# Who reads the output's, k's and q's products out of PSUM: ScalarE alone, with VectorE's share added in SBUF

## The chip, the cores and the metric

One core of a Trainium2 chip runs the whole program. The metric is the device time of one execution in microseconds, as a median of runs. Engines are named as the profile names them: PE (TensorE's matmuls), PEld (its weight loads), DVE (VectorE), ACT (ScalarE), POOL (GpSimd) and SP (SyncE, which here only issues DMAs).

## The reference

Two attention blocks are applied in turn to 8 images of 512 channels and 32 x 32 positions (S = 1024 tokens), all in float32.

```
for each of the two layers:
    xn  = group_norm(x, 8 groups)                  # over channels and positions
    q, k, v = Wq xn + bq, Wk xn + bk, Wv xn + bv   # 512 x 512 matrices
    for each of 8 heads (64 channels):
        a   = softmax(q^T k / 8) over the 1024 keys
        out = a v
    x = x + Wp out + bp
```

## The kernel before

**Jobs.** One image in one layer is a job; there are 16, in the order image 0 layer 0, image 1 layer 0, image 0 layer 1, image 1 layer 1, then the next two images. They are counted from 0. A job's life is: v products (`v_phase`), a phase of products that this text calls the deep phase (`deep_phases`), attention (`Attention.run`), and then the next job's v products. The deep phase of job n computes the output projection of job n - 1 and then k and q of job n. Job 0's has only k and q. `DEEP_V` is 99, so v never runs in the deep phase, and everything that the code does under `with_v` or `n >= DEEP_V` is not reached.

**Products.** Each 512 x 512 by 512 x 1024 multiplication is done with a seven-product scheme (Strassen's, in Winograd's form), applied twice. The outer seven are *chains*, the inner seven are the products of a chain: one matmul of 128x128 weights on 128x256 each, which the profile shows as two records. A deep phase has 21 chains (O, K, Q, seven each in the order `OUTER` = 1, 2, 6, 5, 7, 3, 4), so 147 products. Chains are counted from 0 to 20 here. Two chains are interleaved: product j of chain c stands at place 7c + 2j.

**One chain** has four PSUM banks, z, y, u and w, and takes its products in the order 1, 5, 6, 2, 7, 3, 4 (`chain`, L497 and L501). Product 1 goes to z, and ScalarE copies z to y. Product 5 goes to w, and ScalarE copies it to a small SBUF tile `s5` (L827): this is the product shared by two quarters. Product 6 is added in z, and ScalarE copies z to u. Product 2 completes y, product 7 z, product 3 u and product 4 z again; after each of these four, `put` takes a quarter of the result out of PSUM. For products 2 and 4 ScalarE does it (L816, or L818 with a bias), for products 7 and 3 VectorE, which adds s5 in the same instruction (L823, or L825 with a bias). The next product that goes to a bank waits for the read before it. The last chain of a phase has an order of its own, and half of it goes another way (L820, L821).

**After a chain** (`end`), its result stands in a tile p of the pool `epool` or in its place in k or q. The outer seven results are added up on VectorE: `add` for p into p, k or q (L839), `more` for p into x (L888). Where `more` is called with `moved`, GpSimd issues a DMA that adds p into x (L886). A p tile is free after its last such use. `epool` has 12 buffers: six for p tiles (`PARTS`) and six for weights fetched ahead (`RING`, `fetch`, L188 and L194), which `used` asks for 2.5 us, by the kernel's own clock, after a chain's end.

**Order.** PE, ACT and DVE run in program order (`manual_schedule`), so where Python emits an instruction is where it runs on its engine. The kernel keeps a clock: 0.432 us for each product (`takes`), and `later` puts a step at a time on it. VectorE's work in a deep phase is emitted one item after each product 7 and 3: first `soon` (sums of the moving matrices: four `early` ones for k, then those of output chains 5 and 6, `outs.steps`), then `outer` (the additions above), then `extra`, which holds steps with the first chain at which they may run, such as the next normalisation's statistics (`reads`, from chain 15) and the next image's load (`load_x`, four DMAs at once, from chain 11). What is left of `extra` goes into the first steps of attention. `next_work` and `pump`, which choose by modelled times, are there but used only with `with_v`.

**Weight sums.** `prepare` makes the seven weight factors of a chain with four VectorE instructions (L161 to L167), two chains ahead, the first time that a layer's K and Q are used (jobs 0 and 2); afterwards they come from DRAM ready made (`w<-deep`).

Of the kernel before, what the change touches and what calls it, by code (L numbers as in the profile page):

```python
# [50 lines left out]
AHEAD, TAIL, SLACK, BEHIND, ADD = 0.8, 12.0, 0.6, 1.2, 1.24  # L51
PLACE = {2: (0, 0), 6: (0, 1), 5: (1, 1), 7: (1, 0)}
# [28 lines left out]
def fast_path(  # L81
# [116 lines left out]
    def prepare(key):  # L198
        if key not in raw:
            return  # L200
        raw.discard(key)
        n, which, o = key
        w = held[key]
        for part in range(4):
            factor(w, part)
        keep = wdram.tile([P, NW, P], F32, name=f"deep_{which}_{jobs[n][1]}_{o}")
        deep[which, jobs[n][1], o] = keep
        later(1.0, lambda: nc.sync.dma_start(keep, w))

# [45 lines left out]
    def load_x(b):  # L255
        for cc in range(NC):
            nc.sync.dma_start(xs[b][:, cc, :], x[b, cc * P : (cc + 1) * P, :])

# [375 lines left out]
    def deep_phases(n, extra, outs=None, early=()):  # L634
# [21 lines left out]
        def p_tile(key, name, uses):  # L656
            while len(holds) >= PARTS:
                assert values or outer
                next_work(len(chains), True)
# [6 lines left out]
        def next_work(c, forced=False, limit=None):  # L666
# [9 lines left out]
            if planned and planned[0][1] <= now and not forced:  # L676
                _, _, _, us, fn = planned.popleft()
            elif fits(shared):
# [48 lines left out]
        def begin(c):  # L727
# [7 lines left out]
            if c + 2 < len(chains):  # L735
                ahead, oo = chains[c + 2]
                prepare((job(ahead), ahead, oo))
            if which == O and not with_v and c in (3, 4):
                soon.extend(outs.steps(c + 2))
# [13 lines left out]
            while unread and unread[0] <= c - 3:  # L753
                next_work(c, True)
            s5 = small.tile([P, QT], F32, tag="s5", name=f"s5_{n}_{c}", bufs=3)
# [49 lines left out]
            def put(oo, ph, ps):  # L805
# [8 lines left out]
                if ph == 0:  # L814
                    if b is None:
                        nc.scalar.copy(to_, ps)  # L816
                    else:
                        nc.scalar.activation(to_, ps, AF.Identity, bias=b)  # L818
                elif ends and oo == 1:
                    nc.scalar.activation(to_, ps, AF.Identity, bias=b)  # L820
                    nc.vector.tensor_add(to_, to_, s5)  # L821
                elif b is None:
                    nc.vector.tensor_add(to_, ps, s5)  # L823
                else:
                    nc.vector.scalar_tensor_tensor(to_, ps, b, s5, ALU.add, ALU.add)  # L825
# [3 lines left out]
        def end(c):  # L829
            which, o = chains[c]  # L830
            m = job(which)
            used((m, which, o))
# [4 lines left out]
            def add(to_, a, b, frees):  # L837
                def go():
                    nc.vector.tensor_add(to_, a, b)  # L839
                    let_go((which, frees))  # L840

                ready[go] = clock[0] + BEHIND
                outer.append(go)

            if which == V:
                def add_five():
                    unread.remove(c)
                    to_ = p(o)[:, 2:4, :].rearrange("p t (o c) -> p t o c", o=2)
                    five = fives[V, o].rearrange("p (t c) -> p t c", t=2).unsqueeze(2)
                    nc.vector.tensor_add(to_, to_, five.to_broadcast([P, 2, 2, P]))  # L850

                def plus(to_, a):
# [4 lines left out]
                    ready[go] = clock[0] + BEHIND  # L857
                    values.append((ADD, go))

                unread.append(c)  # L860
                if c < 2:
                    add_five()
                    spend(0.72)
                else:
                    ready[add_five] = clock[0] + BEHIND
                    shared.append((0.72, add_five))
# [7 lines left out]
            if which == O:  # L874
# [3 lines left out]
                def more(oh, sh, part, moved=False):  # L878
# [20 lines left out]
                    ready[go] = clock[0] + BEHIND  # L899
# [12 lines left out]
                elif o == 6:  # L912
                    add(p(6), p(6), p(1), 1)
# [4 lines left out]
                elif o == 7:  # L918
                    add(p(7), p(7), p(6), 6)
# [7 lines left out]
            for to_, a in {  # L927
                2: ((2, 1),), 6: ((6, 1),), 7: ((7, 6), (6, 5), (5, 7)), 3: ((6, 3),), 4: ((7, 4),),
            }.get(o, ()):
                add(p(to_), p(to_), p(a), a)  # L930
# [3 lines left out]
        soon, outer = deque(early), deque()  # L934

        def thunk(i, c, j):
            def go():
                if with_v and not began:
                    began.append(clock[0])
                    free_at[0] = clock[0] + TAIL  # L940
# [4 lines left out]
                if with_v:  # L945
                    if chains[c][0] != V and order[j] in (7, 3):
                        spend(0.38)
                    pump(c, limits[i] and clock[0] + limits[i])
                elif order[j] in (7, 3):
                    if soon:  # L950
                        soon.popleft()()
                    elif outer:
                        outer.popleft()()
                        while outer and outer[0] in free:
                            outer.popleft()()
                    elif extra and extra[0][0] <= c:
                        extra.popleft()[1]()
                if j == 6:
                    end(c)
                    if c + 1 == len(chains):  # L960
                        while outer:
                            outer.popleft()()
                        assert not shared and not values and not planned
# [20 lines left out]
        for c, j in reversed(at):  # L984
            limits.append(limit)
            if chains[c][0] != V and (LAST_ORDER if c + 1 == len(chains) else ORDER)[j] == 7:
# [549 lines left out]
    for n in range(-1, len(jobs)):  # L1536
        last = n + 1 == len(jobs)
        outs = None
        if n >= 0:
# [46 lines left out]
            else:  # L1586
# [7 lines left out]
                elif n >= DEEP_V:  # L1594
                    for i, fn in enumerate(reads):
                        put(3 + i, fn)
                    at = (18, 25, 26, 28, 30, 31, 33, 35, 37, 39)
# [12 lines left out]
                if n + 1 >= DEEP_V:  # L1610
                    for at, fn in zip((41, 43, 45, 47, 49, 51, 53, 55), deep_first):
# [5 lines left out]
                def begin_plan():  # L1617
                    extend_plan(n + 1)
                    for _ in range(RING):
                        fetch()  # L1620

                put(61 if n + 1 < DEEP_V else 56, begin_plan)
# [314 lines left out]
```

## Time and profile before

| what | value |
|---|---|
| median of 3 runs | 3215.66 us (3212.3 to 3217.05) |
| the profiled execution | 3215.82 us, of which the span is 3214.0 us |
| TensorE busy | 3188.8 us (99%), granted clock 0.998 |
| VectorE busy | 2519.1 us (78%) |
| ScalarE busy | 1912.8 us (60%) |
| GpSimd busy | 278.9 us (9%) |
| DMA | 426.45 MB, mean 133 GB/s |
| one deep phase, job 4 | 63.1 us (828.0 to 891.1) |
| one attention, job 4 | 110.0 us (891.1 to 1001.1) |
| v products, job 4 | 24.7 us (803.3 to 828.0) |

How to read it: a line of a timeline has the start in us from the span's start, the length in us, the engine, the line of the kernel, the operation, the tiles written and read, and the shape; in brackets, how long the engine was idle before it, and what ended that. A line of the groups has the shape, the count, the busy time in all, the mean in ns, and the idle time before it with what ended it. A line of the sums by window has the window, its length, the busy time of PE, PEld, DVE, ACT and POOL with the number of instructions, the granted clock, the share of the DMA engines and GB/s. Matmul records overlap: the next starts before the one before it ends, so the pace is the distance between starts.

### The profile page before, as it was taken

To read this page: it belongs to the slowest core of one execution; us is meant where nothing else is said; L and a number is where in the kernel's file an instruction comes from. 1 tells how busy PE (TensorE), PEld (TensorE's weight loads), DVE (VectorE), ACT (ScalarE), POOL (GpSimd) and SP (SyncE) were. 2 spreads that over 40 slices of the span, in tenths; PEclk is the share of its full clock that TensorE was granted. 3 is DMA by queue.
4 is the path that set the end of the run, shared out by engine and by line. 5 is a ranking of instruction groups with operands and counts; after the bars stand their busy time and mean duration, and the time that the engine had idled before them with its cause. 6 is when DMAs were issued, how large, how long until landed. Compare 5 with 4: busy or idle time off the path is not lost.

```text
span 3214.0 us, 58182 instructions
## 1 busy us (share of the span) xinstructions
PE 3188.8 (99%) x22917; PEld 1868.0 (58%) x22917; DVE 2519.1 (78%) x3718; ACT 1912.8 (60%) x3063; POOL 278.9 (9%) x318
## 2 busy tenths in 40 slices
PE   9999999999999999999999999999999999999998
PEld 7366384663846638366483754837557374573844
DVE  8697897867878688786887878778787787877857
ACT  4746646466565665656656565565656656566563
POOL 0100001001010000100001000010000100001000
PEclk9999999999999999999999999999999999999999
DMA  7646565555645354455554535446446463445643
GB/s 273 146 133 161 119 198 146 129 166 110 199 80 136 95 120 137 87 147 143 125 171 94 153 85 124 117 92 178 119 119 174 94 176 61 123 115 102 194 92 76
DMA packets 189561, 426.45 MB, mean 133 GB/s; under 512 B 37736, under 2 KB 63712, under 8 KB 189280
## 3 DMA queue, kind: packets, MB, share of 16 engines
q1 hardware_dynamic: 140432, 273.23, 26.4%
q0 software_dynamic: 48848, 149.44, 25.3%
q8 instruction: 181, 2.97, 0.4%
q14 instruction: 100, 0.82, 0.1%
HBM read 228.15 MB, written 43.84 MB: 85 GB/s over the span
## 4 chain that ended last, share of the span: by engine, by line
PE 90%; DVE 5%; DMA 3%; issue 1%; SPq 0%; ACT 0%; POOL 0%; DVEq 0%; ACTq 0%; POOLq 0%
PE sc L1097 25%; PE po L1148 25%; PE vd L800 10%; PE zd L800 10%; PE z L553 7%; PE yd L800 5%; PE ud L800 4%; PE y L553 2%; PE u L553 2%; PE v L553 2%; DVE acc L1118 1%; DMA x<-p 1%; DMA r<-r 1%; DVE acc L1128 1%; DMA deep<-round 0%
## 5 line engine op out<-in xcount | busy, mean ns | idle before, releaser
L1102 ACT ACTIVATE e<-sc 128x1024 f32<-128x1024 f32 x1024 | 1043.7, 1023 | 566.5 <-PE sc L1097 525.1
L1148 PE MATMUL po<-e,v 64*64 64x512 f32 x8192 | 1059.0, 590 | 2.2 <-ACT e L1102 2.2
L1097 PE MATMUL sc<-q,k 64*64 64x512 f32 x8192 | 1058.7, 590 | 0.0
L1148 PEld LDWEIGHTS po<-e,v 64*64 64x64 f32 x8192 | 313.5, 133 | 568.2 <-issue 544.5
L1097 PEld LDWEIGHTS sc<-q,k 64*64 64x64 f32 x8192 | 311.7, 133 | 562.1 <-issue 523.0
L1118 DVE TENSOR_TENSOR acc<-acc,e 128x1024 f32<-128x1024 f32 x320 | 390.6, 1221 | 67.0 <-ACT e L1102 60.0
L1116 DVE TENSOR_TENSOR acc<-e,e 128x1024 f32<-128x1024 f32 x128 | 156.8, 1225 | 255.1 <-ACT e L1102 255.0
L1125 POOL DMA_DIRECT2D e<-e x224 | 192.6, 860 | 1771.6 <-ACT e L1102 1364.4
L1128 DVE TENSOR_TENSOR acc<-acc,e 128x1024 f32<-128x1024 f32 x224 | 272.9, 1218 | 7.7 <-DMA e<-e 4.6
L800 PE MATMUL zd<-deep,w 128*128 128x256 f32 x860 | 242.1, 381 | 2.3 <-DVE p L823 1.9
L800 PE MATMUL vd<-deep,w 128*128 128x256 f32 x804 | 225.0, 381 | 2.8 <-DVE p L823 0.8
L800 PEld LDWEIGHTS zd<-deep,w 128*128 128x128 f32 x860 | 163.8, 191 | 26.3 <-DVE p L823 3.1
L800 PEld LDWEIGHTS vd<-deep,w 128*128 128x128 f32 x804 | 152.8, 191 | 25.6 <-DVE p L823 1.2
L1183 DVE TRANSPOSE_TENSOR_REDUCE r<-acc 128x32 f32<-128x1024 f32 x128 | 159.2, 1244 | 3.8
L886 POOL DMA_DIRECT2D x<-p x61 | 72.9, 1195 | 949.2 <-ACT p L816 669.7
L1171 DVE TENSOR_TENSOR q<-po,px 128x512 f32<-128x512 f32 x128 | 87.9, 687 | 73.2 <-ACT px L1169 71.7
L800 PE MATMUL vd<-os,w 128*128 128x256 f32 x420 | 117.7, 379 | 0.0
L553 PE MATMUL z<-w,t 128*128 128x256 f32 x480 | 111.0, 379 | 0.0
L553 PE MATMUL z<-w,xn 128*128 128x256 f32 x480 | 110.9, 385 | 0.0
L577 ACT COPY v<-z 128x512 f32<-128x512 f32 x32 | 18.7, 585 | 148.7 <-PE z L553 148.7
L553 PEld LDWEIGHTS z<-w,xn 128*128 128x128 f32 x480 | 90.8, 192 | 24.6 <-PE po L1148 11.4
L501 ACT COPY ud<-zd 128x256 f32<-128x256 f32 x156 | 55.7, 357 | 76.6 <-PE zd L800 75.6
(274 smaller groups left out, 4295.0 us busy)
## 6 DMA issues: line engine op xcount, KB each, us to landing
w<-deep SPq DMA_DIRECT2D x301, 448.0 KB, 4.5
e<-e POOLq DMA_DIRECT2D x224, 512.0 KB, 4.7
x<-p POOLq DMA_DIRECT2D x61, 512.0 KB, 6.3
rb<-rd SPq DMA_DIRECT2D x96, 256.0 KB, 3.8
w<-keep SPq DMA_DIRECT2D x76, 256.0 KB, 5.1
w<-wqkv_dram SPq DMA_DIRECT2D x57, 256.0 KB, 4.7
x<-x_dram SPq DMA_DIRECT2D x28, 512.0 KB, 4.8
out_dram<-x SPq DMA_DIRECT2D x28, 512.0 KB, 4.7
```

The costliest lines, as they stand in the source:

```text
L553: nc.tensor.matmul(ps[:, ti * CH : (ti + 1) * CH], right(src, tx[0], o)[:, cc, t0 : t0 + P], w[:, cc, :], start=(start and ti == 0 and cc ...
L800: nc.tensor.matmul(ps, lhs[:, FACTOR[i], :], moving[i], start=start, stop=True, skip_group_check=True,)
L886: nc.gpsimd.dma_start(to_, p(part), accum_op=ALU.add)
L1097: nc.tensor.matmul(sc[h * HD : (h + 1) * HD, j, :], k[r, hp, k0 : k0 + HD], q[r, hp, sh * HALF : (sh + 1) * HALF], start=True, stop=True,)
L1102: nc.scalar.activation(e, sc, AF.Exp, scale=SCALE)
L1116: nc.vector.tensor_add(acc[g], self.es[i - 1], e)
L1118: nc.vector.tensor_add(acc[g], acc[g], e)
L1125: nc.gpsimd.dma_start(self.summed[i], self.summed.pop(i - 1), accum_op=ALU.add)
L1128: nc.vector.tensor_add(self.acc[g], self.acc[g], self.summed.pop(i))
L1148: nc.tensor.matmul(po[g][j * HD : (j + 1) * HD, h, :], v[r, kc, d0 : d0 + HD], e[r, j, :], start=(kc == 0), stop=(kc == NT - 1),)
L1171: nc.vector.tensor_add(to_, p[:, 1, :], px)
L1183: nc.vector.tensor_reduce(self.r[:, 0, m, :], self.acc.pop(g).rearrange("p j (b e) -> p (j b) e", e=RP), AX.X, ALU.add, apply_transpose=True,)
```

## The change

It does four things. What stands under `with_v` or `n >= DEEP_V` is changed too but not reached, and is left out here.

1. `put`: ScalarE reads all four quarters out of PSUM, the two of products 7 and 3 without s5. Only in the last chain of a phase does it stay as it was.
2. `end`: a chain's s5 is now added by one VectorE instruction to both quarters at once in SBUF (`add_five`, 128x512). All that was done at a chain's end (additions into p, k, q and x, and the accumulating DMAs) is now called after `add_five` has been emitted (`follow`).
3. VectorE's work in every deep phase is chosen by `next_work`: items are emitted while the modelled end of what was emitted lies under 0.8 us (`AHEAD`) ahead of the kernel's clock. The order is `soon`, then `shared` (the `add_five` items, from 1.2 us after the chain's end), then `outer`, then `extra`; modelled prices are 0.75, 0.72, 1.24 and 0.65 us, and 0.9 for `prepare`. `soon` items that a chain needs, and an `add_five` that is three chains old (`FIVES`), are emitted at the latest when that chain begins.
4. The next image's load is four steps of one DMA each, from chains 15, 16, 17 and 18, still ahead of the statistics in `extra`.

```diff
@@ prepare
-            return
+            return False
...
         later(1.0, lambda: nc.sync.dma_start(keep, w))
+        return True
@@
+    def load_steps(b):
+        def chunk(cc):
+            if cc == 0:
+                x_tile(b)
+            nc.sync.dma_start(xs[b][:, cc, :], x[b, cc * P : (cc + 1) * P, :])
+        return [(15 + cc, lambda cc=cc: chunk(cc)) for cc in range(NC)]
@@ next_work
+            elif soon and not forced:
+                us, fn = 0.75, soon.popleft()[1]
             elif fits(shared):
                 us, fn = shared.popleft()
@@ begin
-                prepare((job(ahead), ahead, oo))
+                if prepare((job(ahead), ahead, oo)):
+                    spend(0.9)
             if which == O and not with_v and c in (3, 4):
-                soon.extend(outs.steps(c + 2))
+                soon.extend((c + 2, fn) for fn in outs.steps(c + 2))
+            while any(for_ <= c for for_, _ in soon):
+                soon.popleft()[1]()
+                spend(0.75)
@@ put
                 to_ = e[:, oo, ph * QT : (ph + 1) * QT]
                 b = bias(oo)
-                if ph == 0:
-                    if b is None:
-                        nc.scalar.copy(to_, ps)
-                    else:
-                        nc.scalar.activation(to_, ps, AF.Identity, bias=b)
-                elif ends and oo == 1:
+                if ends and ph == 1 and oo == 0:
+                    nc.vector.scalar_tensor_tensor(to_, ps, b, s5, ALU.add, ALU.add)
+                elif b is None:
+                    nc.scalar.copy(to_, ps)
+                else:
                     nc.scalar.activation(to_, ps, AF.Identity, bias=b)
+                if ends and ph == 1 and oo == 1:
                     nc.vector.tensor_add(to_, to_, s5)
-                elif b is None:
-                    nc.vector.tensor_add(to_, ps, s5)
-                else:
-                    nc.vector.scalar_tensor_tensor(to_, ps, b, s5, ALU.add, ALU.add)
@@ end
+            if c + 1 == len(chains):
+                follow(c)
+                return
+            def add_five():
+                unread.remove(c)
+                five = fives[which, o]
...
+                    to_ = tiles[which, o][:, :, QT:]
+                    five = five.unsqueeze(1)
+                    nc.vector.tensor_add(to_, to_, five.to_broadcast([P, 2, QT]))
+                follow(c)
+            unread.append(c)
...
+                ready[add_five] = clock[0] + BEHIND
+                shared.append((0.72, add_five))
+        def follow(c):
             which, o = chains[c]
             m = job(which)
@@ thunk
-                elif order[j] in (7, 3):
-                    if soon:
-                        soon.popleft()()
-                    elif outer:
-                        outer.popleft()()
-                        while outer and outer[0] in free:
-                            outer.popleft()()
-                    elif extra and extra[0][0] <= c:
-                        extra.popleft()[1]()
+                if c + 1 == len(chains) and order[j] in (7, 3):
+                    spend(0.45)
+                pump(c, limits[i] and clock[0] + limits[i])
                 if j == 6:
                     end(c)
                     if c + 1 == len(chains):
-                        while outer:
-                            outer.popleft()()
+                        while shared or values or outer:
+                            next_work(c, True)
@@ after each job's attention
             if jobs[n][1] == 1 and jobs[n][0] + 2 < B:
-                extra.append((11, lambda b=jobs[n][0] + 2: (x_tile(b), load_x(b))))
+                extra.extend(load_steps(jobs[n][0] + 2))
```

## The prediction

> **What bounds the kernel now.** I read first the page's busy times and chain:
>
> ```profile
> PE 3188.8 (99%) x22917; PEld 1868.0 (58%) x22917; DVE 2519.1 (78%) x3718; ACT 1912.8 (60%) x3063; POOL 278.9 (9%) x318
> PE 90%; DVE 5%; DMA 3%; issue 1%; SPq 0%; ACT 0%; POOL 0%; DVEq 0%; ACTq 0%; POOLq 0%
> ```
>
> TensorE is busy for 99% of a 3214.0 us span: nothing gains here unless it ends a TensorE wait. So I asked, in the stage that the change edits (output, k and q products, one phase for each job; jobs and chains count from 0), for sums by window: job 0, then jobs 1 to 5.
>
> ```profile
> 37.20:82.40 45.20, 43.03 (x196) 36.37 (x194) 41.90 (x106) 26.95 (x70) 0.00 (x0) 1.00 0.72 259
> 223.20:287.20 64.00, 63.36 (x293) 55.28 (x291) 48.45 (x80) 40.38 (x105) 4.79 (x4) 1.00 0.48 133
> 422.00:490.60 68.60, 65.37 (x293) 54.49 (x291) 61.98 (x144) 40.26 (x105) 4.77 (x4) 1.00 0.65 197
> 626.10:693.20 67.10, 65.16 (x293) 56.33 (x291) 47.49 (x79) 40.49 (x105) 5.99 (x5) 0.97 0.67 197
> 828.00:891.10 63.10, 63.10 (x293) 55.35 (x291) 48.39 (x80) 40.49 (x105) 4.77 (x4) 1.00 0.65 201
> 1025.80:1089.00 63.20, 63.20 (x297) 55.42 (x296) 48.44 (x80) 40.41 (x105) 4.77 (x4) 1.00 0.49 133
> ```
>
> The columns are length, then busy time of PE, PEld, DVE, ACT, POOL. Where nothing stalls, a phase takes 63.1 us for 146 products (two matmul records each), 0.432 us a product; jobs 4 to 15 are all within 0.2 us of that. Job 0 has 98 products, 42.3 us at that pace, and takes 45.2. The stage's whole loss is thus 2.9 + 0.9 + 5.5 + 4.0 = 13.3 us, 0.4% of the time, in four phases of sixteen. What ends the waits there, from TensorE's timeline of jobs 2 and 3 and the chain of waits of job 3:
>
> ```profile
> 441.11 0.70 PE L800 MATMUL zd<-os,w 128*128 128x256 f32 x2 [0.85 <-ACT yd L497]
> 448.89 0.70 PE L800 MATMUL zd<-deep,w 128*128 128x256 f32 x2 [0.63 <-DVE p L823]
> ...
> 649.13 11.51 DMA x<-p
> 660.66 3.80 DMA out_dram<-x
> ...
> 666.28 8.64 DMA w<-deep
> ...
> 674.97 0.80 PE vd L800 x2
> ```
>
> Jobs 0 and 2 wait for VectorE's late reads of PSUM (the second line is one of some twelve): VectorE also makes weight sums there and is busy 41.9 of 45.2 us and 62.0 of 68.6. Job 1 and the first line wait for ScalarE, which itself waits for a buffer. Job 3 waits for weights, queued on SP behind output stores, which wait for an 11.5 us accumulating DMA, and then behind the four loads of the next image.
>
> **The change, part by part.** *Reads of products 7 and 3.* Of each chain of seven products ScalarE read five and VectorE two; now ScalarE reads all seven (the last chain of a phase stays as it was). Rows of ScalarE's groups: 0.372 us for a copy, 0.473 with a bias. Two more of these in each of 20 chains are 20 x 2 x 0.43 = 17 us of ScalarE a phase, 40.5 + 17 = 57.5 of 63.1. That is close, so what matters is the distance between starts. Job 4, ScalarE's timeline:
>
> ```profile
> 847.18 0.47 ACT L818 ACTIVATE p<-vd,out_step 128x256 f32<-128x256 f32 x1
> 847.62 0.47 ACT L818 ACTIVATE p<-yd,out_bias 128x256 f32<-128x256 f32 x1
> 848.10 0.36 ACT L497 COPY yd<-zd 128x256 f32<-128x256 f32 x1
> ```
>
> Instructions of 0.47 us start 0.44 apart, at TensorE's pace, and one overlaps the next; in the whole trace the least distance after such a one is 0.37 us. One read per 0.432 us product fits. The Trainium skill (TensorEngine Tiling (Array Packing), section PSUM Bottleneck) says to use both ScalarE and VectorE for emptying PSUM, which speaks against this change and would make the sum that of rival (c). By the rows it fits, and I go by the rows. With the VectorE reads gone, so is their wait: 2.9 us in job 0 and 4.4 of job 2's 5.5. VectorE stays nearly as loaded in these two, and its lag now reaches TensorE through the three s5 tiles (three chains, some 9 us, of cover) and the weight sums (made two chains ahead, 6 us). I take 2.5 and 4.2; bounds 0 and 7.3 together.
>
> *The added sum.* VectorE adds s5 to 128x512 in SBUF. Nearest rows: 128x256 takes 0.419 us (p<-p,s) and 128x1024 1.216; on that line 0.69. It replaces two reads of 0.42 to 0.48: VectorE does 0.2 us less a chain, beside other work: 0. The quarter is now complete only after this add, so everything behind it is later by its wait and length, 0.06 + 0.69 = 0.75 us: the adds into k and q (not needed at once) and, on POOL's queue, the DMA that accumulates p into x. That matters at one place. In each ordinary phase chain 0's DMA goes first, chain 1's waits for it (same part of x), and chain 5 writes its first quarter into chain 1's p buffer. The row of that write, in the groups by form, and the write in job 5 and in job 2:
>
> ```profile
> L818 ACT ACTIVATE p<-yd,out_step 128x256 f32<-128x256 f32 x15 | 7.1, 473 | 6.5 <-DMA x<-p 3.3 <-PE ud L800 1.8 <-PE zd L800 1.0
> ...
> 1042.97 0.47 ACT L818 ACTIVATE p<-yd,out_step 128x256 f32<-128x256 f32 x1 [0.59 <-DMA x<-p]
> ...
> 440.31 0.47 ACT L818 ACTIVATE p<-yd,out_step 128x256 f32<-128x256 f32 x1 [1.80 <-PE ud L800]
> ```
>
> At pace it starts 16.6 us into a phase; chain 1's DMA lands 15.7 to 17.4 us in (jobs 3 to 15). In job 2 it started 1.74 us late (the DMA had landed at 440.2, whatever the line names) and TensorE's next gap was 1.0 us, the stall at 441.11; up to 0.7 us late, the other phases lose nothing. So about 0.73 us are tolerated. With both DMAs 0.75 us later, the landings of jobs 3 to 15 give starts of 16.6 to 18.2 us: seven of the thirteen exceed the tolerance by 0.45 to 0.85, plus 0.1 each to get going again, together 4.7 us. Job 2 loses 0.8 more. Bounds: 0, if the pool gives chain 5 another buffer (chain 0's is now free by then too, since its add no longer stands behind the output sums), and 25, if the DMAs move by 2.5 us. I take 5.5, the value of the nearest row. Job 1's wait is for the same kind of buffer, but there the add into x and with it the DMA come forward, from 16 us into the phase to about 9: 0.9 gained.
>
> *The order by modelled time.* VectorE's items enter its program when its modelled backlog is under 0.8 us, no longer one after each product 7 and 3. Adding the diff's own prices over a normal phase: 20 x 0.72 + 21 x 1.24 + 8 x 0.75 (four of them really 1.13 by the 1.22 us rows) + 9 x 0.65 + 0.9 = 53.2 of 63.5, so nothing is squeezed out, and the statistics, which now end partly in attention, end in the phase. Cost 0; the cover is VectorE's 14.7 idle us (63.1 - 48.4). In job 2 twelve further weight sums of 0.93 fill that room; eight statistics items are left to attention, and the group sums follow their gather after one step instead of five. There VectorE may wait for the gather's DMAs with attention's sums queued behind it: 0 to 2 us for TensorE, I take 0.5.
>
> *Next image in four parts.* Four DMA issues (0.42 us each on SP) leave their place ahead of five weight loads in job 3 and go, one a chain, to chains 15 to 18, behind nearly all weight loads of the phase. The 2 MB no longer share the DMA engines with the load that ended at 674.9. That load took 8.6 us; the median w<-deep takes 4.5. So it would land about 4 us earlier, or 5.9 with the 1.8 us of issues. The wait of 1.94 us goes. What follows it goes too:
>
> ```profile
> 675.55 1.92 PE L800 MATMUL zd<-deep,w 128*128 128x256 f32 x4
> 677.26 1.06 PE L800 MATMUL ud<-xn,w 128*128 128x256 f32 x2
> ```
>
> Four matmul records in 1.71 us are 0.43 a record, half pace, for some 3 us: 1.6 us lost. The skill (TensorE: Matmul & The Clock Gate, section Part 1: The HAM clock gate) puts the drop after an idle window of about 3.4 us; here a 1.94 us gap was followed by it. By the rule alone this part would bring 2.2 us, by the row 3.8. I take 3.5 of the row's. Each step is also charged 0.65 us to VectorE without work there: 2.6 us of its idle time in six phases, four statistics items moved into attention: 0.
>
> **Sum**, against the profiled 3215.8 us (span 3214.0 and 1.8 around it; the median of the runs is 3215.7, the same): 2.5 + 0.9 + 4.2 + 3.5 = 11.1 gained, 5.5 + 0.5 = 6.0 given back. 3215.8 - 5.1 = 3210.7.
>
> **Rivals.** (a) Chain 5 gets another buffer: the 5.5 vanish, and job 2's remaining 1.1 too: 3215.8 - 11.1 - 1.1 + 0.5 = 3204. For: the pool picks by who is free, and job 2's counterpart in job 1 got a weight's buffer. Against: jobs 3 to 15 all have the wait's pattern. (b) Slower, by the same buffer: the DMA of chain 1 lands over 2 us later, because the add on VectorE waits in order behind other items. With 2.5 us, thirteen phases lose 1.9 each: 25 - 11 = +14, 3230. It decides from landings at 18.4 us into the phase on average. Against: VectorE is through with its four first sums at 4.2 us, before chain 0 ends at 4.45. (c) ScalarE becomes the bound: if its 0.473 us reads did not overlap and each cost 0.07 between, a biased chain would take 4 x 0.54 + 3 x 0.43 = 3.45 us against 3.02, 12 chains in 15 phases: +77, 3290. The 0.44 us starts speak against it. (d) It does not do what it says: VectorE's lag in jobs 0 and 2 stalls TensorE through s5 and the weight sums as it did through PSUM, and the small gains meet the small losses: 3215.
>
> **How the numbers follow.** Forecast 0.46, (a) 0.22, (b) 0.17, (c) 0.03, (d) 0.12. 0.2% is 6.4 us, about what a measurement of this kernel can tell from no change: faster is below 3209.3. The forecast's own spread (3204 to 3217) puts two fifths there, (a) nearly all: 0.40 faster. Slower is (b), (c) and the forecast's tail: 0.21. The range from 3201 to 3224 leaves out (c), most of (b) and a little below.
>
> **What would show it.** Right: no TensorE wait for VectorE's p, k or q left at the products' line; job 0's phase near 42.7 us, job 2's near 65, job 3's near 63.6 with no wait for w<-deep; jobs 4 to 15 between 63.1 and 64, with short waits on yd where ScalarE waited for x<-p. Wrong: a phase of 63.1 everywhere (then a), over 64.5 in ordinary phases (b), ScalarE starts over 0.44 apart in a row (c), or stalls in jobs 0 and 2 that now name s5 or w (d).

## The result, and the profile after

| kernel | median | ratio to the kernel before, 95% |
|---|---|---|
| before, beside the first runs | 3214.6 us (6 runs) | |
| changed | 3231.7 us (6 runs) | 1.0051 [1.0038, 1.0064] |
| changed, in a later series | 3228.8 us (4 runs), before 3213.9 (21 runs) | 1.0042 [1.0027, 1.0058] |

The change makes the kernel about 16 us slower, where 5 us less were forecast; 3231.7 us lies above the range. The profiled execution took 3232.4 us (span 3230.6). Its busy times show the work that moved, as expected: ScalarE 1913 to 2160 us, VectorE 2519 to 2488.

```profile
PE 3192.1 (99%) x22917; PEld 1866.6 (58%) x22917; DVE 2488.1 (77%) x3405; ACT 2159.6 (67%) x3689; POOL 283.7 (9%) x318
```

The same sums by window as before the change: the deep phases of jobs 0, 2, 3, 4 and 5, and then job 2's attention (window, length, busy time of PE, PEld, DVE, ACT and POOL, clock, DMA share, GB/s).

```profile
38.60:80.50 41.90, 41.90 (x195) 36.54 (x193) 37.23 (x86) 36.44 (x96) 0.00 (x0) 1.00 0.80 280
422.90:487.60 64.70, 63.70 (x297) 54.95 (x295) 55.19 (x115) 53.85 (x145) 4.77 (x4) 1.00 0.70 208
632.80:695.90 63.10, 63.10 (x295) 55.19 (x293) 43.10 (x56) 56.27 (x145) 5.99 (x5) 1.00 0.70 209
830.60:893.70 63.10, 63.10 (x293) 55.24 (x292) 43.94 (x57) 56.46 (x145) 4.77 (x4) 1.00 0.66 201
1028.50:1095.70 67.20, 65.03 (x293) 56.28 (x291) 45.89 (x62) 56.30 (x145) 4.77 (x4) 0.97 0.47 125
487.60:605.40 117.80, 112.08 (x1025) 38.80 (x1024) 91.42 (x115) 72.92 (x76) 17.25 (x15) 0.99 0.57 136
```

Jobs 0, 2 and 3 got shorter as forecast. Job 4 is untouched, job 5 lost 4.1 us, and job 2's attention went from 110.0 to 117.8. TensorE's longest waits (in total, times, longest):

```profile
PE zd L817 <- ACT yd L508: 10.8, 7, 2.2
PE po L1163 <- ACT e L1117: 8.8, 2, 5.3
PE v L564 <- DVE q L1186: 3.7, 4, 1.9
PE sc L1112 <- ACT e L1117: 2.2, 3, 1.1
```

VectorE's reads and w<-deep are gone from the list. In their place: seven waits for yd in deep phases (the six below and job 2's), and waits in attention. Two profiles of each kernel were taken; means of the two, in us:

| place | before | changed | difference | predicted |
|---|---|---|---|---|
| job 0, deep phase | 45.2 | 42.0 | -3.2 | -2.5 |
| job 0, attention | 113.4 | 118.2 | +4.9 | 0 |
| job 1, deep phase | 64.0 | 63.1 | -0.8 | -0.9 |
| job 2, deep phase | 68.6 | 64.7 | -3.9 | -3.4 (-4.2 + 0.8) |
| job 2's attention and the v products behind it | 135.4 | 146.4 | +11.0 | +0.5 |
| job 3, deep phase | 65.4 (67.2; 63.7) | 63.1 | -2.3 | -3.5 |
| jobs 5, 6, 9, 10, 13, 14, deep phases | 378.9 | 392.4 | +13.5 | +4.7 in jobs 3 to 15 |
| span | 3211.9 | 3230.0 | +18.1 | -5.1 |

The lines above the span add up to 19.2; the other -1.1 us are scattered. So three questions: why just these six phases, why job 2's attention, why job 0's.

**The six phases.** They are those of jobs 3 to 15 whose output belongs to layer 0. Job 5, ScalarE's write of chain 5's first quarter, SP's issue of a weight before it, and then TensorE's timeline behind it:

```profile
1048.14 0.47 ACT L836 ACTIVATE p<-yd,out_step 128x256 f32<-128x256 f32 x1 [3.12 <-DMA x<-p]
```

```profile
1040.27 0.32 SPq L189 DMA_DIRECT2D w<-deep  x1
```

```profile
1048.94 0.70 PE L817 MATMUL zd<-os,w 128*128 128x256 f32 x2 [2.17 <-ACT yd L508]
...
1050.57 1.06 PE L817 MATMUL zd<-xn,w 128*128 128x256 f32 x2
1051.42 1.06 PE L817 MATMUL zd<-os,w 128*128 128x256 f32 x2
```

The write comes 3.1 us late, because chain 1's accumulating DMA (x<-p) still reads that buffer; TensorE stands for 2.17 us and then runs at half pace for a while. Half pace followed in three of the twelve phases of the two profiles, which lost 4.1 to 4.3 us each; the other nine lost 1.0 to 2.4. This is the wait the prediction named. But the DMA was not issued late: in job 5 11.0 us into the phase in both kernels, over the six phases and both profiles 11.06 against 10.88 on average. It took longer, 7.9 us against 6.2. What the DMAs did from 11 to 20 us into job 5, before and then changed (KB each, median us from issue to landing):

```profile
w<-deep SPq DMA_DIRECT2D x2, 448.0 KB
x<-p POOLq DMA_DIRECT2D x1, 512.0 KB, 6.0
```

```profile
w<-deep SPq DMA_DIRECT2D x3, 448.0 KB
x<-p POOLq DMA_DIRECT2D x1, 512.0 KB, 8.6
```

The third weight of the second list is not the point: it went out 18.85 us into the phase, when the DMA was nearly done. The first one is. It is K's fifth weight (the one of outer product 5), which used to wait for the buffer of chain 3's weight and went out 13.15 us into the phase; now it goes at 11.79 (the SP line above, 1040.27 - 1028.48), because it takes chain 0's p buffer, which VectorE's new order frees early. The first addition of output tiles, which frees it, in the changed kernel and then before:

```profile
1039.02 1.23 DVE L879 TENSOR_TENSOR p<-p,p 128x1024 f32<-128x1024 f32 x1 [0.17 <-ACT p L834]
```

```profile
1040.63 1.22 DVE L839 TENSOR_TENSOR p<-p,p 128x1024 f32<-128x1024 f32 x1
```

It starts 10.54 us into the phase instead of 14.79, and its end at 1040.25 lets the fetch go. The list of buffers in the built programs shows the exchange: before, K's fifth weight follows chain 3's weight and chain 6's p follows chain 0's p; changed, the two are crossed. Chain 5's p follows chain 1's p in both. What the earlier fetch does to the DMA shows in the queues over the first 3 us after its issue (packets, MB, share of the DMA engines; q0 carries GpSimd's DMAs, q1 SP's), before and then changed:

```profile
q1 hardware_dynamic: 144, 0.46, 50.2%
q0 software_dynamic: 103, 0.21, 39.9%
```

```profile
q1 hardware_dynamic: 193, 0.63, 87.4%
```

Before, chain 1's DMA had moved 0.21 MB by then; in the changed kernel it had moved nothing, as two weights one behind the other kept the engines busy. In job 4 the DMAs of the same stretch, changed kernel, read:

```profile
w<-deep SPq DMA_DIRECT2D x3, 448.0 KB
x<-p POOLq DMA_DIRECT2D x1, 512.0 KB, 5.0
out_dram<-x SPq DMA_DIRECT2D x1, 512.0 KB
```

There a layer-1 output is stored; the store, ahead on SP's queue, waits for the accumulating DMA itself, so the weights go out only after it has landed, and it lands in 5.0 us. That is why the other phases lose nothing.

### The profile page after: what moved, and what is told of

The parts are those of the page before. It is cut to its first block, busy times and chain, and to the rows that moved or that the text cites. A ratio compares the mean times of both kernels' runs of the same rounds, so it can differ in the third digit from the quotient of the medians.

```text
span 3230.6 us, 58790 instructions
## 1 busy us (share of the span) xinstructions
PE 3192.1 (99%) x22917; PEld 1866.6 (58%) x22917; DVE 2488.1 (77%) x3405; ACT 2159.6 (67%) x3689; POOL 283.7 (9%) x318
## 5 line engine op out<-in xcount | busy, mean ns | idle before, releaser
L859 DVE TENSOR_TENSOR p<-p,s 128x512 f32<-128x512 f32 x185 | 127.3, 688 | 86.9 <-ACT p L834 49.0
L588 ACT COPY v<-z 128x512 f32<-128x512 f32 x32 | 18.8, 586 | 148.7 <-PE z L564 148.7
L859 DVE TENSOR_TENSOR k<-k,s 128x512 f32<-128x512 f32 x64 | 44.2, 691 | 91.4 <-ACT k L836 48.6
```

The costliest lines, as they stand in the source:

```text
L859: nc.vector.tensor_add(to_, to_, five.to_broadcast([P, 2, QT]))
```

## Experiments

The theory after the result: (1) the fetch, let in 1.4 us earlier, stretches chain 1's accumulating DMA, and chain 5 waits for its buffer; (2) job 2's attention loses because group sums stand right behind their gather; (3) job 0's attention was open. Rivals: the add of s5 delays the DMA, VectorE's order as such, or ScalarE being full. "Six phases" below are those of jobs 5, 6, 9, 10, 13 and 14, and their loss is the sum over 63.12 us each.

**The parts alone.** Only the load in four steps:

```diff
 kernel before
-                extra.append((11, lambda b=jobs[n][0] + 2: (x_tile(b), load_x(b))))
+                extra.extend(load_steps(jobs[n][0] + 2))
```

> The kernel before, with only the next image's load as four steps in chains 15 to 18. If the gain of 4.1 us seen in job 3 comes from this part alone, job 3's deep phase goes from 67.2 to 63.1-63.6 us here and no w<-deep wait is left in it, all other deep phases stay within 0.3 us, and the run is 3.5 to 4.1 us under the kernel before (about 3211). Rival: without the order by modelled time the four steps push statistics out of the phase into attention, and an attention behind such a phase (jobs 3, 4, 7, 8, 11, 12) grows by over 1 us: then the run is level with before or above it.

Measured: 3214.1 against 3214.6 us, ratio 1.000 [0.999, 1.0009]. Job 3's phase was 63.12, but the run gained nothing. Part of the reason showed when the kernel before was profiled again:

> The kernel before once more, for a second profile: job 3's w<-deep wait and jobs 0 and 2's waits on VectorE again, 2.9 and 5.5 and 4.0 us; job 0's attention anywhere from 113 to 119, by the same small DMA.

```profile
PE vd L800 <- DMA w<-deep: 1.2, 3, 0.7
```

Job 3 took 63.7 us there, with the same instructions: three waits of at most 0.7 us and no drop of the clock, in place of one of 1.9 and 1.6 us of half pace. The 4.1 us of the first profile were mostly that execution's own: with the load in one step and without the order by modelled time, job 3's phase also took 64.1 us in rd_later, 63.4 in reads_early_add and 63.1 in reads_only, all below. Besides, the profile of load_parts_only lost 3.0 us in the v products behind job 1's attention, which the edit does not reach. Also, the four loads hardly moved: 38.7 to 40.5 us into the phase, against 38.4 to 39.7, since SP's queue stands behind output stores until some 35 us; one weight more (nine, not eight) goes ahead of them. The rival's spilled statistics were there (VectorE waited 4.8 to 5.7 us for the gather in attention of jobs 3, 4, 7, 8, 11 and 12) and cost 0.2 us at most.

Only the order by modelled time; `put` is that of the kernel before, and so is the load. (Left out below: the additions get the delay that the s5 additions had, and VectorE's work is held back ahead of its reads of PSUM in every chain, not only the last.)

```diff
 changed kernel
@@ end
-            if c + 1 == len(chains):
+            if which != V:
                 follow(c)
                 return
@@ thunk
-                if c + 1 == len(chains) and order[j] in (7, 3):
-                    spend(0.45)
+                if order[j] in (7, 3):
+                    spend(0.38)
```

> The kernel before, with only the order of VectorE's items by modelled time; VectorE still reads products 7 and 3, the load is still one step. Theory (the shared buffer): in the built program K's fifth weight still takes the buffer of chain 3's weight, as before, so it is fetched 13.1 us into a phase, chain 1's accumulating DMA lands by 17.5 us and the deep phases of jobs 5, 6, 9, 10, 13, 14 stay at 63.1-63.3 us, against 64.4-67.3 with the whole change. Rival (the order by itself makes the chain 5 wait): these six lose together over 8 us here too. For job 2's attention: if the order alone leaves its statistics over, attention and the v products behind it are 7 to 10 us longer here as in the changed kernel; if it takes ScalarE's reads too, under 2 us.

Measured: 3246.0 us, ratio 1.0099 [1.0082, 1.0116], slower than the whole change. Not six but all ordinary phases lost, 64.4 to 65.9 us each, so this is another wait. VectorE in job 5:

```profile
1042.27 1.22 DVE L497 TENSOR_TENSOR deep<-xn 128x1024 f32<-128x1024 f32 x1
1043.41 1.22 DVE L499 TENSOR_TENSOR deep<-xn,deep 128x1024 f32<-128x1024 f32 x1
1044.54 0.42 DVE L840 TENSOR_TENSOR p<-vd,s 128x256 f32<-128x256 f32 x1
```

Four early sums of 1.22 us, priced at 0.75, stand ahead of the first PSUM read, and TensorE waits 1.03 us for it. So at these prices the order needs ScalarE's reads. Job 2's attention took 119.2 us, with eight statistics left over and a wait of 9.1 us for the gather: that loss comes with the order alone.

Only ScalarE's reads, the s5 addition ahead of the one item after each product 7 or 3 (the load is that of the kernel before):

```diff
 changed kernel
-                pump(c, limits[i] and clock[0] + limits[i])
+                if order[j] in (7, 3):
+                    if shared:
+                        shared.popleft()[1]()
+                    if soon:
+                        soon.popleft()[1]()
+                    elif outer:
...
```

> ScalarE reads all four quarters and VectorE adds s5 in SBUF, one such add ahead of the item after each product 7 or 3; the order is else that of the kernel before, and so is the load. Theory (the shared buffer): K's fifth weight keeps the buffer of chain 3's weight, is fetched 13.1 us into a phase, chain 1's DMA lands by 17.5 us, and the six phases of jobs 5, 6, 9, 10, 13, 14 lose under 3 us together. Rival (the prediction's price: the add delays the DMA): both accumulating DMAs are issued some 0.75 us later than before and jobs 3 to 15 lose about 5 us. Rival (ScalarE is the bound): every ordinary phase is over 64 us. Job 0's phase 42.0-43.0 us, as VectorE's reads of PSUM are gone, job 2's 65 or less; job 3 keeps its w<-deep wait (66.5-67.5).

Measured: 3213.0 us, 0.9997 [0.9988, 1.0007]; the six phases lose 0.0, the buffers are as in the kernel before, chain 1's DMA lands at 17.0 to 17.2 us in the six phases. Job 0's phase was 43.3 and job 1's 63.1. ScalarE alone keeps TensorE's pace, and the s5 addition by itself costs nothing: both rivals fall. Three of the expected phases were missed: job 0's by 0.3 us, job 2's, which kept 68.0 (the reads alone do not take away its waits), and job 3's, which took 63.1 with its load in one step.

**The fetch, both ways.** In the changed kernel, chain 0's buffer is freed later:

```diff
 changed kernel
                     add(6, 1, 1)
+                    ready[outer[-1]] = clock[0] + 6.0
```

> The changed kernel, with one edit: the first addition of the output's sums (chain 2's result plus chain 0's) is put into VectorE's program no earlier than 6 us of modelled time after it was queued. It frees chain 0's buffer later, so in the built program K's fifth weight again takes the buffer of chain 3's weight, and is fetched 13.1 us into a phase instead of 11.8. Theory (the shared buffer): in the phases of jobs 5, 6, 9, 10, 13, 14 chain 1's DMA lands by 17.5 us instead of 18.4-19.6, and their 14.7 us of loss fall to under 4; the run is 10 to 14 us under the changed kernel, 3218 to 3222. Rival (the DMA is long because the change issues it against other work of VectorE or POOL, not because of the weight): landings and the six phases stay as in the changed kernel, 3230 or more.

Measured: 3210.2 us, 0.9987 [0.9977, 0.9996]: some 20 us under the changed kernel. The six phases lose 0.1 us. The fetch and the DMAs of job 5's stretch, and ScalarE's write:

```profile
1033.41 0.32 SPq L189 DMA_DIRECT2D w<-deep  x1
```

```profile
w<-deep SPq DMA_DIRECT2D x2, 448.0 KB
x<-p POOLq DMA_DIRECT2D x1, 512.0 KB, 6.1
```

```profile
1037.48 0.47 ACT L836 ACTIVATE p<-yd,out_step 128x256 f32<-128x256 f32 x1 [0.68 <-DMA x<-p]
```

The fetch is at 13.15 us again (1033.41 - 1020.26) and the DMA, issued at the same 11.0 us, takes 6.1 instead of 8.6. The run fell by more than the 13.5 of the six phases; its attentions of jobs 0 and 2 were also shorter by 3 us each in this execution.

The other way round, in reads_only, which has nothing of the new order, chain 0's buffer is freed early:

```diff
 reads_only
                     add(6, 1, 1)
+                    outer.pop()()
```

> reads_only with one edit: the first addition of the output's sums is put into VectorE's program right behind chain 2's s5 addition. Nothing of the order by modelled time is in it, but in the built program K's fifth weight now takes chain 0's buffer, as in the changed kernel, and is fetched about 11.8 us into a phase. Theory (the fetch stretches chain 1's accumulating DMA): that DMA is issued as in reads_only (10.7-10.9 us) but lands at 18.0-19.6 instead of 17.0-17.2 us in the phases of jobs 5, 6, 9, 10, 13, 14, which lose 6 to 15 us together; the run is 3219 to 3228 against reads_only's 3213. Phases of jobs 4, 7, 8, 11, 12, where SP's queue stands behind a store, stay at 63.1. Rival (the loss needs the order by modelled time): no phase over 63.4 and the run at 3213.

Measured: 3221.1 us, 1.0022 [1.0013, 1.0031], 8 us over reads_only. The fetch is at 11.79 us, chain 1's DMA (issued at 10.6 to 11.0) lands at 18.1 to 18.8, and the six phases lose 8.0 us; jobs 4, 7, 8, 11 and 12 none. Chain 1's DMA in job 5, in reads_only and then with the line:

```profile
x<-p POOLq DMA_DIRECT2D x1, 512.0 KB, 6.4
```

```profile
x<-p POOLq DMA_DIRECT2D x1, 512.0 KB, 7.8
```

In job 4 and its like the addition is as early, but the store holds the fetches back until the DMA has landed. One line of order, in a kernel without the rest, brings the wait back: theory (1) is shown.

Chain 0's result added by VectorE, so that chain 1's DMA starts early:

```diff
 changed kernel
-                    more(0, 0, 1, m > 0)
+                    more(0, 0, 1)
```

> The changed kernel, with one edit: the output's first chain is added into x by VectorE in every job (as it already is in job 1's phase) instead of by an accumulating DMA, so chain 1's DMA has none to wait for and is issued some 8 to 9 us into a phase instead of 11. K's fifth weight still takes chain 0's buffer. Theory (chain 5 waits for chain 1's buffer): chain 1's DMA lands before 16.6 us, ScalarE's 2 to 3 us waits at chain 5's first write go, the phases of jobs 5, 6, 9, 10, 13, 14 are 63.1-63.4 us and job 2's under 64; job 2's attention keeps its loss; the run is 3213 to 3218. Rival (VectorE has no room for one more 1.2 us addition): ordinary phases over 63.6 us and statistics left over in more jobs.

Measured: 3215.4 us, 0.9997 [0.9987, 1.0007]. The fetch is still at 11.79, but chain 1's DMA is issued at 8.8 and lands at 13.8 to 16.1; the six phases lose nothing (job 2's took 64.2, a little over the 64). Job 3's rose to 66.5, with its old wait for a weight back:

```profile
681.62 0.70 PE L817 MATMUL vd<-t,w 128*128 128x256 f32 x2 [2.24 <-DMA w<-deep]
```

Job 3's next accumulating DMA now met a store and three weights: issued at 14.0 us, it landed at 24.2, SP's queue stood behind a store that waits for it, and later weights came late.

**Job 2's attention.** The group sums further behind the gather:

```diff
 changed kernel
-                at = (10, 19, 22, 24, 26, 28, 36, 39, 42, 45)
+                at = (15 if len(extra) > 4 else 10, 19, 22, 24, 26, 28, 36, 39, 42, 45)
```

> The changed kernel, with one edit: where more than four steps are left over for attention (job 2's), the group sums follow at the fifteenth step instead of the tenth, six steps behind the gather. Theory (VectorE stands idle for the gather's DMA in an attention that has no time to spare): no wait for the gather is left, attention of job 2 and the v products behind it go from 117.9 and 27.3 us to 110-112 and 25, the run is 7 to 10 us under the changed kernel, 3222 to 3225; chain 5's waits stay. Rival (the eight statistics items and what POOL does between are the cost, not the wait): attention of job 2 stays over 114 us.

Measured: 3217.4 us, 1.0007 [0.9997, 1.0018]; attention of job 2 is 110.0 and the v products behind it 24.9. Chain 5's waits stayed (13.2 us). The group sums in the changed kernel and then here:

```profile
512.50 0.22 DVE L335 BATCH_NORM_STATS2 gs<-gm 8x6 f32<-8x64 f32 x1 [5.42 <-DMA gm<-dm]
```

```profile
515.89 0.21 DVE L335 BATCH_NORM_STATS2 gs<-gm 8x6 f32<-8x64 f32 x1
```

So theory (2) holds for the attention: its 7.9 us hang on VectorE's 5.4 us wait. The 3 us of the v products behind it went too, but came back in a run below that has no such wait (held_sums_18), so their cause stays open. Nor is the price fixed: with the group sums in the old place job 2's attention lost 4.9 us behind a wait of 4.9 in first_add_held, and 2.8 behind one of 5.6 in first_by_vector. Why such a wait cost nothing in load_parts_only is read from the busy times 30 to 70 us into the attentions of jobs 2 and 3, kernel before:

```profile
520.60:560.60 40.00, 40.00 (x376) 14.17 (x372) 30.94 (x41) 28.81 (x31) 5.14 (x6) 1.00 0.74 195
723.25:763.25 40.00, 40.00 (x376) 14.24 (x372) 28.51 (x38) 28.81 (x31) 5.14 (x6) 1.00 0.48 95
```

Job 2's attention also makes a round of weight sums (VectorE busier, DMA share 0.74 against 0.48). By this reading, which no run tests, the lag is not worked off there: GpSimd's next e<-e DMAs come late, VectorE waits for one of those in turn (4.84 us at 523.86 in the changed kernel), and the end of attention pays:

```profile
601.28 1.94 ACT L1117 ACTIVATE e<-sc 128x1024 f32<-128x1024 f32 x2 [5.57 <-DVE acc L1143]
```

```profile
602.36 3.15 PE L1163 MATMUL po<-e,v 64*64 64x512 f32 x16 [3.50 <-ACT e L1117]
```

**Both together.** The held addition with the later sums, the VectorE addition with the later sums, and the held addition with the sums at the eighteenth step. The first two join edits shown above; the third is

```diff
 first_add_held
                 at = (10, 19, 22, 24, 26, 28, 36, 39, 42, 45)
+                if len(extra) > 4:
+                    at = (18, 22, 24, 26, 28, 30, 36, 39, 42, 45)
```

> The changed kernel with the first addition held (K's fifth weight back at 13.1 us) and the group sums of job 2 six steps behind the gather. If the two losses are the two that make the change slower, and independent: first_add_held's 3210.2 less 4 to 6, about 3205, 9 to 11 us under the kernel before. Rival (they share a cause): no better than 3209.

> The changed kernel with the output's first chain added by VectorE and the group sums of job 2 six steps behind the gather. It also takes job 2's own wait at chain 5 (1.5 us): if VectorE has room for the addition, 3203 to 3206, at or under the variant that holds the first addition. Rival (no room on VectorE): 3208 or more, with phases over 63.6 us.

> The changed kernel with the first addition held and the group sums of job 2 at the eighteenth step, the later steps of the normalisation at 22 to 30. VectorE's 3.2 us wait for the gather, left in held_sums_later, goes; if the 2.4 us lost in the v products of job 3 hang on it, 3204 to 3206; if not, as held_sums_later, 3208.

Measured: 3208.2 us, 0.9975 [0.9966, 0.9984]; 3208.9, 0.9981 [0.9971, 0.9991]; and 3211.4, 0.9988 [0.9979, 0.9997]. All three lie under the kernel before, the first by the most. None reached its lower figure: held_sums_later kept a 3.2 us wait for the gather and 27.4 us of v products behind job 2's attention, vector_sums_later 64.3 in job 3, and all three had 118.2 to 118.7 us in job 0's attention. Taking the 3.2 us wait away (held_sums_18) left the 27.4 (TensorE waits 2.4 us there for VectorE's q): they did not hang on it.

**Job 0's attention.** A second profile of the changed kernel:

> The changed kernel once more, unedited, for a second profile. Theory: the six phases and job 2's attention lose again (14 and 8 us, each within 3), as they are in the program's order. Job 0's attention (117.4 us against 113.5) is expected to follow the landing of one small DMA (rd<-rt, 1.4 to 4.0 us) and can come out anywhere from 114 to 119.

It lost 12.5 us in the six phases, 7.9 in job 2's attention and 4.1 in the v products behind it, and job 0's attention took 119.1. In that attention POOL issues a 512 KB e<-e and SP, at nearly the same time, the 8 KB rd<-rt that the softmax normalisation waits for. Kernel before, and then changed:

```profile
157.15 0.87 POOL L1125 DMA_DIRECT2D e<-e  x1 [9.43 <-ACT e L1102]
157.65 0.35 SPq L1223 DMA_DIRECT2D rd<-rt  x1
159.34 0.63 SPq L1225 DMA_DIRECT2D rb<-rd  x1
```

```profile
155.22 0.87 POOL L1140 DMA_DIRECT2D e<-e  x1 [9.43 <-DVE lt L1225]
155.85 0.35 SPq L1238 DMA_DIRECT2D rd<-rt  x1
...
158.84 1.29 SPq L1240 DMA_DIRECT2D rb<-rd  x2
```

rb<-rd goes when rd<-rt has landed: 1.69 us after it, or 2.99. All 16 profiles of this study fall in two groups: rd<-rt issued 0.18 to 0.50 us after e<-e, next step after 1.4 to 1.7 us (five profiles); issued 0.58 us or more after it, 3.0 to 4.0 us (eleven). Job 0's attention took 113.2 to 116.5 us in the five and 117.4 to 119.6 in the eleven. So two small VectorE instructions were put ahead in the kernel before, to push rd<-rt back:

```diff
 kernel before
+    nc.vector.tensor_max(lmax, lmax, lt)
+    nc.vector.tensor_max(rmax, rmax, inv)
     for i in range(2):
         nc.vector.transpose(rt[:, i, :], inv[:, i, :])
...
-    nc.vector.tensor_max(lmax, lmax, lt)
-    nc.vector.tensor_max(rmax, rmax, inv)
```

> The kernel before, with the two small VectorE maxima (0.11 and 0.13 us) that stand behind the two transposes of the softmax sums put ahead of them: rd<-rt is issued some 0.2 us later, nothing else is changed. Theory (race of two DMAs): the small DMA now falls behind the packets of POOL's accumulating e<-e, lands 3 to 4 us after its issue instead of 1.4 to 1.7, and job 0's attention goes from 113.2-113.5 to 117-119 us; the run is 3 to 5 us over the kernel before, about 3218. Rival (VectorE has too much to do there in the new order): attention of job 0 under 114.5 and the run level with the kernel before.

```profile
157.53 0.87 POOL L1125 DMA_DIRECT2D e<-e  x1 [9.43 <-ACT e L1102]
158.81 0.35 SPq L1227 DMA_DIRECT2D rd<-rt  x1
...
162.30 2.01 SPq L1229 DMA_DIRECT2D rb<-rd  x2
```

Measured: issued 1.28 us after e<-e, followed 3.49 us later, attention 117.7 us instead of 113.4, as the race says. (It was pushed by more than the edit's 0.2 us: the gather before it also landed later.) But the run was level, 3213.6 us, 0.9997 [0.9988, 1.0007]. What an execution without a profile does there can't be seen; that the kernel before also falls on the late side in some of its runs (3211 to 3219 us) would explain it and is not shown. The last experiment missed:

```diff
 held_sums_later, put_first
-                moves[at] = start
+                moves[at + (n == 0)] = start
```

> held_sums_later with one edit: in job 0's attention the raw weights' load is issued one step later, behind the gather of the softmax sums instead of ahead of it on SP's queue, so rd<-rt goes out some 1.5 us earlier and ahead of POOL's e<-e. Theory (race of two DMAs): rd<-rt lands 1.4 to 1.7 us after its issue, job 0's attention is 112 to 114 us instead of 118.5, the run 3 to 5 us under held_sums_later's 3208. Rival (VectorE has too much to do there): attention of job 0 stays over 116.5 us.

Measured: 3210.3 us, 0.9984 [0.9975, 0.9993], attention 119.2. The raw weights still stood ahead of the gather on SP's queue (142.41 and 145.08 us), so the edit did not move what it was to move and tells nothing of the race.

## Why the prediction was wrong

**The bound, and the gains: right, with one caveat.** TensorE's waits were where the prediction had them. Job 0 gained 3.2 (2.5 predicted), job 1 0.8 (0.9), job 2 3.9 (3.4). Job 3's 3.5 was read from one execution; over two it is 2.3, and the load in parts alone moved no median. The load was said to go "behind nearly all weight loads"; in fact it stayed in its place in time and let one more weight ahead. Rival (d), that the change does nothing, is out.

**ScalarE and the added sum: right.** One read per 0.432 us product fits, and the new VectorE instruction takes the 0.69 us that were interpolated:

```profile
L859 DVE TENSOR_TENSOR p<-p,s 128x512 f32<-128x512 f32 x185 | 127.3, 688 | 86.9 <-ACT p L834 49.0 <-ACT p L836 36.6 <-DMA out_dram<-x 0.6
```

The Trainium skill (TensorEngine Tiling (Array Packing), section PSUM Bottleneck) asks, where tiling has sped TensorE up, for both ScalarE and VectorE to empty PSUM. Here ScalarE alone kept up, at 56.3 of 63.1 us in job 3's phase.

**Chain 5's wait: right place, wrong size.** Same buffer (rival (a) was wrong), and the tolerance of 0.73 us was nearly right: in reads_only and first_add_held starts 0.64 us late cost nothing, 0.70 cost 0.07 and 0.84 cost 0.21. The step that failed is "with both DMAs 0.75 us later, the landings of jobs 3 to 15 give starts of 16.6 to 18.2". It carried over the duration that the DMA had before. The issue moved by 0.2 us (chain 0's DMA, which it waits for, was itself shorter); the duration went from 6.2 to 7.9 us, in the phases that have no store on SP's queue, because a weight fetch let in 1.4 us earlier went ahead of it. The term was 4.7 and measured 13.5: six phases of 2.3 us, not seven of thirteen by 0.5 to 0.9. The prediction noted that chain 0's buffer would be free earlier and asked only whether chain 5 would take it; it did not ask who else would.

**Rival (b)** had the size: it said landings over 2 us late and 3230 us; in the six phases they came 1.9 us late on average (19.0 against 17.1). Its cause, the addition waiting in order on VectorE, was wrong: chain 1's s5 addition ended 7.44 us into the phase, as in reads_only, and its DMA was issued 0.2 us later than before.

**Job 2's attention: the term was 0.5 and measured 11.0.** The prediction had the event (group sums one step behind their gather, VectorE waiting, attention's sums queued behind), and put "0 to 2 us for TensorE" on it without a row of job 2's attention. Of the 11.0, attention's 7.9 are shown to follow from that wait; the rest, in the v products, is open.

**Job 0's attention** had no term: +4.9 us, more than job 0's deep phase gained. In the profiles it goes with a step of 0.1 us between two DMAs; the one edit that was to undo it did not move them, so the cause is shown only in part.

Put together afterwards, with these three terms as measured, the prediction's own sum would have been 11.1 - 0.8 - 13.5 - 11.0 - 4.9, or 19 us slower, against 18.1 between the profiles.

## What to carry to other kernels

When an edit reorders who frees a buffer, follow the pool: the next tile in line may be a transfer that starts earlier, and an early transfer is not free if it gets ahead of one that something waits for. Carry over where a transfer starts, but work its length out anew from what now runs beside it. A stall seen in one profiled execution is worth a second profile before it is booked as a gain, and a wait that one stage hides (0.2 us for 5 us of VectorE's) can cost more than its length in another (7.9 for 5.4).

## What the runs showed of the hardware

An accumulating DMA of 512 KB within SBUF took 5.0 to 5.4 us with no weight fetch beside it, 5.8 to 6.4 when, with one 448 KB weight fetch under way, the next was issued 1.9 us or more behind it, and 7.1 to 8.6 when that next one was issued 0.6 to 1.2 us behind it. An 8 KB DMA that the normalisation waits for released its follower after 1.4 to 1.7 us or after 3.0 to 4.0, depending on whether it was issued up to 0.50 us, or 0.58 us and more, behind a 512 KB one on another queue.

TensorE's half pace followed some gaps of about 2 us and not others, and the length of the gap does not tell which. In deep phases it followed gaps of 1.94 us (kernel before), 2.17 and 2.18 (changed) and 2.30 us (its second profile), but not 2.10 us in the latter, nor 2.24 us in first_by_vector. In the v products it followed 1.87 us (second profile of the changed kernel) and not 2.74 (load_parts_only):

```profile
614.53 3.25 PE L564 MATMUL v<-w,t 128*128 128x256 f32 x8 [1.87 <-DVE q L1186]
```

```profile
405.96 1.35 PE L562 MATMUL v<-w,t 128*128 128x256 f32 x5 [2.74 <-DVE q L1180]
```

Eight records took 3.25 us in the one and five 1.35 in the other; the granted clock was 0.50 from 615.1 to 618.5 us, and stayed at 1.00 after the second gap. The Trainium skill (TensorE: Matmul & The Clock Gate, section Part 1: The HAM clock gate) speaks of an idle window of about 3.4 us; the runs show the drop after shorter gaps as well, and the measurement decides.
